# A four-layer GNN stack on one core: when the first layer's norms come, batch norm's coefficients in pieces, and another instruction order

## The chip, the cores and the metric

The kernel runs on one core of one Trainium2 chip. The metric is the device time of one execution in microseconds (us). Engines are named as in the profile: PE is the matrix engine (TensorE) and PEld its weight loads, DVE is VectorE, ACT is ScalarE, POOL is GpSimd, and SP (SyncE) issues most of the DMA transfers.

## The reference

The input x has 128 graphs of 64 nodes with 256 features, in float32; all graphs share one adjacency matrix. Four layers follow one another, each with a residual and a layer norm around it:

```python
def reference(x, adj, ...):
    # layer 0: aggregation, 256 -> 512, batch norm, ReLU, 512 -> 256, batch norm
    x = _layernorm(x + _L0_gnn_ref(x, adj, W1, b1, g1, be1, W2, b2, g2, be2))
    # layer 1: Chebyshev convolution, attention with 4 heads, feed-forward (exact GELU)
    x = _layernorm(x + _L1_gnn_ref(x, adj, adj, ...))
    # layer 2: two graph convolutions, then LSTMs over windows of 1, 2, 3 and 4 nodes
    x = _layernorm(x + _L2_gnn_ref(x, adj, ...))
    # layer 3: graph attention
    return _layernorm(x + _L3_gnn_ref(x, adj, W, a))

def _L0_gnn_ref(features, A, W1, b1, g1, be1, W2, b2, g2, be2):
    ...
    agg = jnp.einsum('nm,bmd->bnd', A_hat, features)
    x = agg.reshape(-1, d)
    h = jax.nn.relu(_batchnorm(x @ W1.T + b1, g1, be1))     # mean and variance over all 8192 rows
    out = h @ W2.T + b2
    return _batchnorm(out, g2, be2).reshape(b, n, -1)
```

Batch norm needs the mean and variance of a feature over all 128 x 64 rows. So layer 0 has two points at which every block must be done before any can go on: bn1 (512 features) and bn2 (256 features).

## The kernel before

**Blocks and tiles.** The 128 graphs are cut into 16 blocks of 8 graphs, 512 rows each. A block's activations are one SBUF tile of 128 partitions by 1024 elements (x, `Xs[i]`; a second one is `Hs[i]`). All matrix products write to four PSUM tiles of 128x1024 (`PS`); eight temporary SBUF tiles of the same size (`mem`, in the profile t) are handed out and returned.

**Layer 0.** `first_block(i)` aggregates block i (L346), multiplies by W1 in two halves of 256 features (L370; a half is 8 records on PE), evicts each to SBUF with the bias on ACT (L589, L591) and takes batch statistics on DVE (L593). The 512 features are four chunks of 128; half 0 is chunks 0 and 1, half 1 chunks 2 and 3. `bn_coeffs` makes scale and shift of bn1 for all four chunks at once: an aggregate for each chunk (L548), an addition (L549), a power on POOL (L551) and three small DVE operations (L553 to L555). `second_block(i)` applies scale, shift and ReLU on ACT (`relu`, L601) and multiplies by W2. Block 0 does that plainly, feature chunk by feature chunk (L611). Blocks 1 to 15 use a scheme with seven half-size products in place of eight (L645), with differences and sums on DVE and POOL and copies out of PSUM on ACT (L657) between them (DVE L664, L668, L669). Then come the statistics for bn2 (L684), and bn2's coefficients.

**Join to layer 1.** `end_block(i)` applies bn2 on ACT (L746, four of 512 elements for two blocks), transposes the block back on PE (L364), adds x (DVE L754) and applies the layer norm: statistics on DVE (L290 to L292), a power on POOL (L313), a small DVE operation (`ln_nm`, L316) and four ACT operations (L319). `block(i)` is layer 1: aggregation (PE L346), a copy (ACT L768), the product by Wc (PE L382), an addition (DVE L777), a layer norm, three elementwise operations (DVE L781 to L783), transposes (PE L358), a copy (ACT L791), the products for Q, K and V (PE L370, L815), attention, and a feed-forward part. ACT switches function tables between exp (L861) and gelu (L935). `at_end` says how many end blocks stand ahead of each block; their order is `ends = (0, 1, 12, 13, 14, 15, 2, 3, ...)`.

**Layers 2 and 3.** `gcn_block(i)` does the two graph convolutions and the first LSTM. `unit` does an LSTM over windows of p = 2, 3 and 4 nodes. Products that depend only on the input are at L1081; the recurrent steps use the same scheme of seven products (L1153), in four stages for each gate, with ACT and DVE work between them (L1221). The last units use plain products (L1289, L1291). `last_block(i)` is graph attention and the output.

**What sets the order.** The order of instructions on PE, DVE, ACT and POOL is fixed when the kernel is built. Each part of the work is a Python generator that yields a step (engine, planned us, PSUM tiles and temporaries to take, and from when), and `flow` runs a planned clock over all the generators: it always emits the step whose planned start is the earliest. A step's margin is multiplied by a pseudo-random number that depends on the stretch of 50 us in which it falls, with one seed for each stretch in `DRAWS`:

```python
soon = max(t if r[6].urgent else t + margin.get(e, 0.0) * drawn(r[0][1], t), free[e])
...
end, now = when + us, when
```

So a planned cost or a draw that changes can change the order of everything after it. The emitted order is what the engines execute, each in its own queue; real waits come from the data.

## Time and profile before

| | |
|---|---|
| time, median of 3 runs (lowest to highest) | 2354.76 us (2354.64 to 2355.97) |
| the profiled execution: time, span | 2355.12 us, 2353.0 us |
| mean granted PE clock | 0.987 |
| PE, DVE, ACT, POOL busy | 2266.4, 1365.9, 1167.2, 435.4 us |
| instructions | 40443 |
| DMA | 57.88 MB, mean 25 GB/s |
| first half of layer 0, bn1, second half | to 149.1, 149.1 to 155.9, to 263.6 us |
| first L364 of layer 1's inputs, first L382 | 268.2, 280.4 us |
| last LSTM product | ends at 2294.85 us |

A line of the timeline gives start, duration, engine, line, operation, output from input, and how many records it joins; in brackets stands the idle time of the engine before it, and what released it. Most float32 products of this kernel leave two records. A stage's row (a window) gives its length, each engine's busy time in it, the mean granted clock of PE, the share of time in which the DMA engines were busy, and their GB/s. In the page's first line the percentages are shares of the span. The chain is the work that ended last, followed back through what released it.

### The profile page before, as it was taken

The page shows a single profiled execution, that of the slowest core. Times are in us where ns is not written, and L with a number is a line of the kernel's source. Part 1 is how long each engine was busy: PE and PEld are TensorE (multiplying, and loading weights), DVE is VectorE, ACT ScalarE, POOL GpSimd, SP SyncE. Part 2 cuts the span into 40 slices and gives each one's busy share as a digit, 9 for nine tenths or more (in the row PEclk, how much of TensorE's full clock was granted, in tenths as well). Part 3 has the DMA queues.
Part 4 walks back from the last instruction along what each step waited for, and adds up shares of the span by engine and source line. Part 5 has one row for each costly group of instructions (what it writes and reads, how often), then busy time and mean ns, then how long its engine had stood idle before and what let it go on. Part 6 is the DMA issues. An engine that isn't in the chain of part 4 may idle for free.

```text
span 2353.0 us, 40443 instructions
## 1 busy us (share of the span) xinstructions
PE 2266.4 (96%) x16916; PEld 1753.1 (75%) x16916; DVE 1365.9 (58%) x2865; ACT 1167.2 (50%) x2257; POOL 435.4 (19%) x322
## 2 busy tenths in 40 slices
PE   8989789999999999999999999999999999999996
PEld 4548666676666676667667888999988888978884
DVE  5557589666766556567544444454454655563567
ACT  2357465644454544445444444444444544653676
POOL 0011124221314224215120100011100111110112
PEclk9999899999999999999999999999999999999998
DMA  6100310000000000101000000000001001000111
GB/s 170 46 1 1 99 60 30 27 10 11 10 10 10 10 11 3 44 2 46 19 19 10 18 1 1 19 1 1 1 1 36 1 10 37 28 10 27 54 37 55
DMA packets 42632, 57.88 MB, mean 25 GB/s; under 512 B 6225, under 2 KB 35537, under 8 KB 42449
## 3 DMA queue, kind: packets, MB, share of 16 engines
q1 hardware_dynamic: 41344, 54.22, 7.2%
q8 instruction: 132, 2.16, 0.4%
q10 hardware_dynamic: 1104, 1.08, 0.1%
q14 instruction: 52, 0.42, 0.1%
HBM read 38.52 MB, written 16.78 MB: 23 GB/s over the span
## 4 chain that ended last, share of the span: by engine, by line
PE 80%; issue 8%; DVE 7%; ACT 4%; POOL 0%; DMA 0%; ACTq 0%; POOLq 0%; DVEq 0%
PE ps L1153 27%; PE ps L1081 14%; PE ps L370 11%; PE ps L382 6%; PE ps L945 4%; PE ps L645 3%; PE ps L346 2%; PE ps L815 2%; PE ps L1532 2%; PE ps L1289 2%; PE ps L1291 2%; PE ps L358 2%; DVE ln_st L290 1%; PE ps L364 1%; DVE ln_mv L291 1%
## 5 line engine op out<-in xcount | busy, mean ns | idle before, releaser
L1153 PE MATMUL ps<-t,x 128*128 128x256 f32 x928 | 226.8, 380 | 0.3 <-DVE x L1221 0.3
L313 POOL TENSOR_TENSOR ln_rs<-ln_rs,neghalf 128x4 f32<-128x4 f32 (+1 forms) x104 | 108.5, 1043 | 610.6 <-DVE ln_rs L292 535.6
L1153 PEld LDWEIGHTS ps<-t,x 128*128 128x128 f32 x928 | 173.0, 190 | 22.8 <-issue 1.6
L1049 ACT ACTIVATE t<-ps,bih 128x512 f32<-128x512 f32 (+5 forms) x185 | 98.2, 568 | 159.7 <-PE ps L1081 103.7
L319 ACT ACTIVATE x<-x,ln_nm,ln_rs 128x256 f32<-128x256 f32 x228 | 118.1, 591 | 66.9 <-DVE ln_nm L316 66.9
L1153 PE MATMUL ps<-x,x 128*128 128x256 f32 x608 | 147.5, 380 | 1.5 <-DVE t L1221 1.1
L1049 ACT ACTIVATE x<-ps,bih 128x512 f32<-128x512 f32 (+5 forms) x159 | 82.2, 548 | 106.3 <-PE ps L1081 67.9
L1153 PEld LDWEIGHTS ps<-x,x 128*128 128x128 f32 x608 | 114.4, 190 | 17.2 <-DVE t L1221 1.8
L370 PE MATMUL ps<-t,W1T 128*128 128x512 f32 x256 | 114.7, 595 | 0.0
L290 DVE BATCH_NORM_STATS2 ln_st<-x 128x6 f32<-128x256 f32 x244 | 97.6, 400 | 0.7
L1049 ACT ACTIVATE x<-x,bih 128x512 f32<-128x512 f32 (+5 forms) x134 | 69.3, 564 | 51.8 <-DVE x L1219 49.7
L1081 PE MATMUL ps<-t,wL 128*128 128x512 f32 x216 | 94.6, 594 | 0.2 <-ACT t L1378 0.2
L291 DVE BATCH_NORM_AGGREGATE ln_mv<-ln_st 128x2 f32<-128x6 f32 x448 | 81.4, 182 | 15.3
L1081 PE MATMUL ps<-h,wL 128*128 128x192 f32 (+2 forms) x456 | 89.6, 352 | 0.6 <-DVE x L1599 0.6
L1081 PE MATMUL ps<-h,x 128*128 128x256 f32 x384 | 86.1, 379 | 0.0
L370 PEld LDWEIGHTS ps<-t,W1T 128*128 128x128 f32 x256 | 46.7, 190 | 48.9 <-issue 48.5
L1081 PEld LDWEIGHTS ps<-h,wL 128*128 128x128 f32 x456 | 69.6, 190 | 17.8 <-issue 16.0
L1212 DVE COPY x<-ps 128x256 f32<-128x256 f32 (+2 forms) x67 | 25.5, 381 | 98.4 <-PE ps L1153 98.4
L1219 DVE TENSOR_TENSOR x<-ps,x 128x512 f32<-128x512 f32 (+2 forms) x67 | 40.8, 609 | 69.3 <-PE ps L1153 64.3
L316 DVE SCALAR_TENSOR_TENSOR ln_nm<-ln_mv,ln_rs 128x4 f32<-128x4 f32 (+1 forms) x104 | 61.4, 593 | 33.2 <-POOL ln_rs L313 33.1
L1081 PEld LDWEIGHTS ps<-h,x 128*128 128x128 f32 x384 | 72.8, 190 | 9.8
L319 ACT ACTIVATE t<-t,ln_nm,ln_rs 128x256 f32<-128x256 f32 x112 | 58.5, 591 | 41.0 <-DVE ln_nm L316 40.9
(692 smaller groups left out, 5374.3 us busy)
## 6 DMA issues: line engine op xcount, KB each, us to landing
t<-in_x_dram SPq DMA_DIRECT2D x28, 512.0 KB, 4.4
xd<-x SPq DMA_DIRECT2D x16, 512.0 KB, 2.6
x<-xd SPq DMA_DIRECT2D x8, 512.0 KB, 3.3
out_dram<-x SPq DMA_DIRECT2D x8, 512.0 KB, 2.9
wL<-in_L_gnn_Wih_dram SPq DMA_DIRECT2D x2, 1024.0 KB, 4.9
x<-in_L_gnn_Whh_dram SPq DMA_DIRECT2D x2, 1024.0 KB, 5.0
wB<-in_L_gnn_W_dram SPq DMA_DIRECT2D x2, 512.0 KB, 4.3
h<-in_x_dram SPq DMA_DIRECT2D x2, 512.0 KB, 4.0
```

The costliest lines, as they stand in the source:

```text
L290: V.bn_stats(st[:, t, :], y[:, t, :])
L291: V.bn_aggr(mv[:, t, :], st[:, t, :])
L313: G.tensor_tensor(rs, rs, neghalf[:, :n], ALU.pow)
L316: V.scalar_tensor_tensor(nm, mv[:, :, 0], -1.0, rs, ALU.mult, ALU.mult)
L319: S.activation(y[:, t, :], y[:, t, :], AF.Identity, scale=rs[:, t : t + 1], bias=nm[:, t : t + 1])
L370: T.matmul(ps[:, c, :], w[:, k, (off + c) * P : (off + c + 1) * P], yT[:, k, :], start=(k == 0), stop=(k == nk - 1),)
L382: T.matmul(ps[:, t, :], yT[:, k, t * P : (t + 1) * P], w[:, k, :], start=(k == 0), stop=(k == nk - 1),)
L645: T.matmul(dst, w[:, k, :], y[:, k, :], start=first and k == 0, stop=k == 1, skip_group_check=not first)
L945: T.matmul(tm(PS[ps])[:, t, :], fm(mem[gs[k // 2]])[:, k % 2, t * P : (t + 1) * P], W2[:, k, :], start=(k == 0), stop=(k == 3),)
L1049: S.activation(dst, z, AF.Tanh, bias=bl[:, p - 1, 2 * g + c : 2 * g + c + 1], scale=(1.0 if g == 2 else 0.5) * (1.0 if p == 1 else 0.5),)
L1081: T.matmul(spread(fm(PS[ps])[:, j, :n], q), WL[p][0][:, k, m], x_of(0, q)[:, k], start=(k == 0), stop=(k == 1),)
L1153: T.matmul(dst, WS[p][name](k, g), y[:, k], start=first and k == 0, stop=k == 1, skip_group_check=not first)
```

## The change

It touches the order in five ways, and the arithmetic of no result. bn1's coefficients are made in two pieces, each as soon as the statistics of its two chunks are there; block 0's ReLUs are planned in pairs, and the other blocks' ReLUs, differences and evictions in smaller steps. (bn2 uses the same function with one piece, and the last block's statistics for it are single steps.) Fifteen of the sixteen blocks leave `end_block` without their layer norm, which is the first thing that `block(i)` then does; block 0 keeps it in `end_block` (`NORMED = range(1)`). Four end blocks in place of two stand ahead of block 0. Planned costs are changed in many steps, and steps that read PSUM are planned from the end of the product, or of the copy, that they wait for. `DRAWS` has 50 other values.

In the kernel before, one function makes all coefficients; after, this one is called for `(0, 2)` and `(2, 4)` of bn1 and `(0, 2)` of bn2:

```diff
+        def bn_coeffs(name, c0, c1, st, g, be, at):
+            sc, sh, mv = (t[:, c0:c1] for t in bn[name])
+            for c in range(c1 - c0):
+                yield step("V", 0.5, at=lambda: at(c0 + c))
+                V.bn_aggr(mv[:, c, :], st[:, c0 + c, :, :].rearrange("p i s -> p (i s)"))
+            yield step("V", 0.2)
             V.tensor_scalar(sc, mv[:, :, 1], EPS, None, ALU.add)
             yield step("G", 1.0)
-            G.tensor_tensor(sc, sc, neghalf[:, :nch], ALU.pow)
+            G.tensor_tensor(sc, sc, neghalf[:, : c1 - c0], ALU.pow)
             yield step("V", 0.6)
...
+        stats_at = lambda c: ready(*[("l0a", c // 2, i) for i in blocks])
+        for c in (0, 2):
+            tasks.append(
+                (
+                    lambda c=c: stats_at(c),
+                    lambda c=c: bn_coeffs("bn1", c, c + 2, st1, cols["g1"], cols["be1"], stats_at),
...
+        tasks += [(lambda i=i: ready(("bn1", 0), *[("bn1", 2)] * (i > 0)), lambda i=i: second_block(i), 2) for i in blocks]
```

In `second_block`:

```diff
             if i == 0:
                 for f in range(4):
-                    yield step("S", 0.7)
-                    relu(f)
-                    yield step("T", 1.75, ps=int(f == 0), waits=f == 3)
+                    if f % 2 == 0:
+                        for j in (f, f + 1):
+                            t_j = yield step("S", 0.65, at=lambda: done.get(("bn1", f)))
+                            relu(j)
+                    yield step("T", 1.75, ps=int(f == 0), at=t_j - 0.65 * (1 - f % 2))
...
-            yield step("S", 2.92)
-            for f in range(4):
-                relu(f)
+            t_x = yield step("S", 1.46)
+            relu(0)
+            relu(1)
...
-            yield step("S", 0.75, waits=False)
+            t = yield step("S", 0.75, at=max(t, t_2))
             S.copy(y[:, 0, :], p[:, 0, :])
             S.copy(y[:, 3, :], p[:, 3, :])
-            t = yield step("T", 1.75)
+            yield step("T", 1.75, at=max(t, t_h))
             product(A12, h[:, :, u], p[:, 2, :])
```

At the join to layer 1:

```diff
     def end_block(i):
...
-        yield step("S", 1.5)
         for c in range(2):
+            yield step("S", 0.7)
...
-        yield from ln_steps_act(x)
+        if i in NORMED:
+            yield from ln_steps_act(x)
         mark("end", i)
 
     def block(i):
         x = X[i]
         mark("begun", i)
+        if i not in NORMED:
+            yield from ln_steps_act(x)
...
-    at_end = {0: 2, 1: 4, 2: 8, 3: 10, 4: 14, 5: 16}
+    at_end = {0: 4, 1: 4, 2: 8, 3: 10, 4: 14, 5: 16}
```

Planned costs and waits, of which these are the LSTM's main ones:

```diff
-        us = n * 1.68e-3
-        v_us, g_us, s_us = (0.08 + n * r for r in (1.15e-3, 2.4e-3, 1.05e-3))
+        us = 0.012 + n * 1.665e-3
+        v_us, g_us, s_us = (0.08 + n * r for r in (1.15e-3, 2.35e-3, 1.0e-3))
+        v2_us, s2_us = 0.07 + n * 2.25e-3, 0.2 + n * 1.68e-3
...
-                at[g, "a"] = yield step("S", copy_us, at=t - us, waits=False)
+                at[g, "a"] = yield step("S", copy_us, at=t, waits=False)
                 S.copy(y[:, 0, :], v[:, 0, :])
...
-                yield step("T", us, at=h_at, waits=False)
+                yield step("T", us, at=max(h_at, at[g, "a"], at[g, "e"]), waits=False)
                 product(g, "A12", h_u, v[:, 2, :])
...
-                at[g, "0"] = yield step("V", two_us, at=at[g], waits=False)
+                at[g, "0"] = yield step("V", two_us, at=t, waits=False)
                 V.tensor_tensor(y[:, 0:2, :], v[:, 2:4, :], y[:, 0:2, :], ALU.add)
```

The rest changes a planned number alone (0.95 to 0.98 for the aggregations, and the gates', for example), or the ordering key `tbl`.

More of the change, by code (lines that the diff above doesn't have):

```diff
@@ L31 @@
 STRETCH = 50.0
-DRAWS = [511, 307, 323, 0, 388, 0, 0, 35, 178, 58, 461, 150, 363, 205, 36, 263, 190, 963, 453, 309, 108, 239, 50, 391, 578, 171, 630, 639, 804, 485, 290, 771, 646, 0, 976, 942, 0, 370, 0, 0, 618, 674, 887, 378, 432, 790, 44, 487, 800, 1]
+DRAWS = [119, 456, 684, 0, 152, 590, 97, 0, 0, 316, 775, 750, 291, 668, 396, 690, 972, 316, 700, 299, 810, 345, 289, 861, 902, 463, 567, 883, 455, 277, 848, 910, 108, 288, 531, 607, 103, 756, 415, 205, 829, 978, 419, 437, 870, 596, 976, 248, 270, 919]
 @with_exitstack
@@ L313, in ln_steps_act @@
         G.tensor_tensor(rs, rs, neghalf[:, :n], ALU.pow)
-        yield step("V", 0.2)
+        yield step("V", 0.2, tbl="m")
         nm = sm.tile([P, n], F32, tag="ln_nm", name="ln_nm")
@@ L539, in eig, with bn_tiles @@
             PS.give(0)
-        def bn_coeffs(name, nch, st, g, be):
-            mv = ctile([P, nch, 2], f"{name}mv")
-            sc = ctile([P, nch], f"{name}sc")
-            sh = ctile([P, nch], f"{name}sh")
-            yield step("V", 0.15 + 0.5 * nch)
-            for c in range(nch):
-                V.bn_aggr(mv[:, c, :], st[:, c, :, :].rearrange("p i s -> p (i s)"))
+        def bn_tiles(name, nch):
+            bn[name] = ctile([P, nch], f"{name}sc"), ctile([P, nch], f"{name}sh"), ctile([P, nch, 2], f"{name}mv")
+        def bn_coeffs(name, c0, c1, st, g, be, at):
[4 more added lines that the diff above has]
+            yield step("V", 0.2)
             V.tensor_scalar(sc, mv[:, :, 1], EPS, None, ALU.add)
             yield step("G", 1.0)
-            G.tensor_tensor(sc, sc, neghalf[:, :nch], ALU.pow)
+            G.tensor_tensor(sc, sc, neghalf[:, : c1 - c0], ALU.pow)
             yield step("V", 0.6)
-            V.tensor_tensor(sc, sc, g, ALU.mult)
+            V.tensor_tensor(sc, sc, g[:, c0:c1], ALU.mult)
             V.tensor_tensor(sh, mv[:, :, 0], sc, ALU.mult)
-            V.tensor_tensor(sh, be, sh, ALU.subtract)
-            bn[name] = sc, sh
-            mark(name)
+            V.tensor_tensor(sh, be[:, c0:c1], sh, ALU.subtract)
+            mark(name, c0)
         st1 = ctile([P, 4, NBLK, 6], "st1", wp)
@@ L569, in first_block @@
                 xs = early[i]
-            yield step("T", 0.95, ps=1, sl=1, tbl="quarter")
+            yield step("T", 0.98, ps=1, sl=1, tbl="quarter")
             ps = PS.take()
@@ L593, in first_block @@
                     V.bn_stats(st1[:, 2 * hf + c, i, :], dst[:, c, :])
-            mark("l0a", i)
+                mark("l0a", hf, i)
         def second_block(i):
-            sc1, sh1 = bn["bn1"]
+            sc1, sh1, _ = bn["bn1"]
             src = [(fm(Xs[i]) if f < 2 else H[i])[:, f % 2, :] for f in range(4)]
@@ L623, in second_block @@
                 return
-            yield step("S", 2.92)
-            for f in range(4):
-                relu(f)
+            t_x = yield step("S", 1.46)
+            relu(0)
+            relu(1)
             x, h = fm(Xs[i]), H[i]
             u, v = slice(0, TB // 2), slice(TB // 2, TB)
-            yield step("V", 1.4, sl=2, tbl="m")
+            t_1 = yield step("V", 0.7, sl=2, at=t_x, tbl="m")
             slots = [mem.take() for _ in range(2)]
@@ L636, in second_block @@
             V.tensor_tensor(T1, x[:, :, v], x[:, :, u], ALU.subtract)
-            V.tensor_tensor(T2, h[:, :, v], T1, ALU.subtract)
-            yield step("G", 1.3, waits=False, tbl="m")
-            G.tensor_tensor(T4, h[:, :, u], T2, ALU.subtract)
-            yield step("V", 0.7, tbl="m")
-            V.tensor_tensor(T3, h[:, :, v], x[:, :, v], ALU.subtract)
+            t_h = yield step("S", 1.46, at=t_x)
+            relu(2)
+            relu(3)
             def product(w, y, dst, first=False):
@@ L649, in second_block @@
             A11, A12, A22 = (W2T[:, k : k + 2, c * P : (c + 1) * P] for k, c in ((0, 0), (2, 0), (2, 1)))
-            yield step("T", 1.75, ps=1)
+            t = yield step("T", 1.75, ps=1, at=t_1)
             ps = PS.take()
@@ L654, in second_block @@
             product(W2S[0], T1, p[:, 3, :], first=True)
-            yield step("S", 0.75, waits=False)
+            t_2 = yield step("V", 0.7, at=t_h, tbl="m")
+            V.tensor_tensor(T2, h[:, :, v], T1, ALU.subtract)
+            yield step("G", 1.3, waits=False, tbl="m")
+            G.tensor_tensor(T4, h[:, :, u], T2, ALU.subtract)
+            yield step("V", 0.7, tbl="m")
+            V.tensor_tensor(T3, h[:, :, v], x[:, :, v], ALU.subtract)
+            t = yield step("S", 0.75, at=max(t, t_2))
             S.copy(y[:, 0, :], p[:, 0, :])
             S.copy(y[:, 3, :], p[:, 3, :])
-            t = yield step("T", 1.75)
+            yield step("T", 1.75, at=max(t, t_h))
             product(A12, h[:, :, u], p[:, 2, :])
@@ L669, in second_block @@
             V.tensor_tensor(y[:, 0:2, :], p[:, 2:4, :], y[:, 0:2, :], ALU.add)
-            yield step("T", 0.88)
+            t_y = Clock.end + LAG
+            t = yield step("T", 0.88)
             product(A22, T4, p[:, 0, :])
@@ L673, in second_block @@
                 mem.give(sl)
-            yield step("S", 1.5, ps=-1)
+            t_h = yield step("S", 0.6, at=t_y)
             S.activation(h[:, 0, :], fm(Xs[i])[:, 0, :], AF.Identity, bias=cols["b2"][:, 0:1])
+            if i == NBLK - 1:
+                yield step("V", 0.65, waits=False)
+                V.bn_stats(st2[:, 0, i, :], h[:, 0, :])
+                mark("l0b", 0, i)
+            yield step("S", 0.4, at=t_y)
             S.activation(h[:, 1, v], y[:, 3, :], AF.Identity, bias=cols["b2"][:, 1:2])
+            yield step("S", 0.4, ps=-1, at=t)
             S.activation(h[:, 1, u], p[:, 0, :], AF.Identity, bias=cols["b2"][:, 1:2])
@@ L681, in second_stats @@
         def second_stats(i):
-            yield step("V", 1.25)
-            for c in range(2):
+            for c in range(i == NBLK - 1, 2):
+                yield step("V", 0.65)
                 V.bn_stats(st2[:, c, i, :], H[i][:, c, :])
-            mark("l0b", i)
+                mark("l0b", c, i)
         blocks = range(NBLK)
@@ L689 @@
         tasks[3:3] = [(None, later_loads, 0)]
-        tasks.append(
-            (
-                lambda: ready(*[("l0a", i) for i in blocks]),
-                lambda: bn_coeffs("bn1", 4, st1, cols["g1"], cols["be1"]),
-                0,
-            )
-        )
-        tasks += [(lambda: ready(("bn1",)), lambda i=i: second_block(i), 2) for i in blocks]
-        tasks.append(
-            (
-                lambda: ready(*[("l0b", i) for i in blocks]),
-                lambda: bn_coeffs("bn2", 2, st2, cols["g2"], cols["be2"]),
-                0,
-            )
-        )
+        bn_tiles("bn1", 4)
+        bn_tiles("bn2", 2)
+        stats_at = lambda c: ready(*[("l0a", c // 2, i) for i in blocks])
[4 more added lines that the diff above has]
+                    lambda c=c: bn_coeffs("bn1", c, c + 2, st1, cols["g1"], cols["be1"], stats_at),
+                    0,
+                )
+            )
+        tasks += [(lambda i=i: ready(("bn1", 0), *[("bn1", 2)] * (i > 0)), lambda i=i: second_block(i), 2) for i in blocks]
+        ends_at = lambda c: ready(*[("l0b", c, i) for i in blocks])
+        tasks.append((lambda: ends_at(0), lambda: bn_coeffs("bn2", 0, 2, st2, cols["g2"], cols["be2"], ends_at), 0))
         flow([Stream(1, 0, [(None, eig, 0)], urgent=True), Stream(6, 1, tasks)], {"T": 2.0})
@@ L731 @@
         V.tensor_tensor(rb2, rb2, be2, ALU.add)
-    sc2, sh2 = bn["bn2"]
+    sc2, sh2, _ = bn["bn2"]
     Wv_par = Wv.rearrange("p k (u r e) -> p k r u e", u=2, r=2)
+    NORMED = range(1)
     def end_block(i):
@@ L762, in block @@
         mark("begun", i)
-        yield step("T", 0.95, ps=1, sl=1, tbl="quarter")
+        if i not in NORMED:
+            yield from ln_steps_act(x)
+        yield step("T", 0.98, ps=1, sl=1, tbl="quarter")
         ps = PS.take()
@@ L829, in block @@
         G.tensor_tensor(y, y, row["bo"], ALU.add)
-        yield step("T", 0.95, ps=1, sl=1, tbl="quarter")
+        yield step("T", 0.98, ps=1, sl=1, tbl="quarter")
         ps = PS.take()
@@ L879, in block @@
         PS.give(ps)
-        yield step("T", 0.95, ps=1, sl=1, tbl="quarter")
+        yield step("T", 0.98, ps=1, sl=1, tbl="quarter")
         ps = PS.take()
@@ L1090, in gates @@
         def gates(pair, t, ps, sl):
-            t = yield step("S", 0.1 + n * 2.5e-3, ps=-1, at=t, waits=False)
+            t = yield step("S", 0.42 + n * 1.64e-3, ps=-1, at=t, waits=False)
             for j, (g, c) in enumerate(pair):
@@ L1147, in lstm @@
         hn = n // 2
-        half_us, two_us = (0.15 + j * hn * 1.05e-3 for j in (1, 2))
+        half_us, two_us = (0.07 + j * hn * 1.08e-3 for j in (1, 2))
         copy_us = 0.15 + hn * 1.0e-3
@@ L1226, in stage4 @@
                 product(g, "A22", T4, v[:, 0, :])
-                yield step("S", 0.1 + n * 1.15e-3, at=at[g, "0"], waits=False)
+                yield step("S", 0.1 + n * 1.03e-3, at=at[g, "0"], waits=False)
                 gate(of(act[g])[:, 0], of(act[g])[:, 0], g, 0)
@@ L1243, in lstm @@
             yield from stage4(2)
-            t_g = yield step("V", 2 * v_us, at=at[2], waits=False, tbl="m")
+            t_g = yield step("V", v2_us, at=at[2], waits=False, tbl="m")
             times(of(act[2]), of(act[0]), of(act[2]))
@@ L1251, in lstm @@
             yield from stage4(1)
-            yield step("V", 2 * v_us, at=at[1], waits=False, tbl="m")
+            yield step("V", v2_us, at=at[1], waits=False, tbl="m")
             times(cell, of(act[1]), cell)
             mem.give(act[1])
-            t = yield step("V", 2 * v_us, at=t_g, waits=False, tbl="m")
+            t = yield step("V", v2_us, at=t_g, waits=False, tbl="m")
             V.scalar_tensor_tensor(cell, cell, 0.5, of(act[2]), ALU.mult, ALU.add)
@@ L1259, in lstm @@
                 mem.give(j)
-            t = yield step("S", 2 * s_us, at=t, waits=False)
+            t = yield step("S", s2_us, at=t, waits=False)
             S.activation(of(act[2]), cell, AF.Tanh, scale=0.5)
-            t = yield step("V", 2 * v_us, at=max(t, at[3]), sl=0 if last else 1, waits=False, tbl="m")
+            t = yield step("V", v2_us, at=max(t, at[3]), sl=0 if last else 1, waits=False, tbl="m")
             if last:
@@ L1291, in products @@
                         T.matmul(dst, WL[p][1][:, k, m], of(s_h)[:, k], start=False, stop=(k == 1))
-                t = yield step("S", 0.3 + n * 2.1e-3, ps=-1, at=t, waits=False)
+                t = yield step("S", 0.42 + n * 1.64e-3, ps=-1, at=t, waits=False)
                 for j, (g, c) in enumerate(pair):
@@ L1331, in gcn_block @@
     def gcn_block(i):
-        yield step("T", 0.95, ps=1, sl=1, tbl="quarter")
+        yield step("T", 0.98, ps=1, sl=1, tbl="quarter")
         ps = PS.take()
@@ L1353, in gcn_block @@
         S.activation(mem[s_h1], mem[s_h1], AF.Relu)
-        yield step("T", 0.95, ps=1, sl=1, tbl="quarter")
+        yield step("T", 0.98, ps=1, sl=1, tbl="quarter")
         ps = PS.take()
@@ L1713 @@
         MARGIN,
-        start=done["bn2",],
+        start=done["bn2", 0],
     )
```

## The prediction

> **What bounds the kernel now.** I read the page first, then PE's waits, then a table of stages, then the timeline at the two joins of layer 0.

> ```profile
> PE 2266.4 (96%) x16916; PEld 1753.1 (75%) x16916; DVE 1365.9 (58%) x2865; ACT 1167.2 (50%) x2257; POOL 435.4 (19%) x322
> ...
> PE 80%; issue 8%; DVE 7%; ACT 4%; POOL 0%; DMA 0%; ACTq 0%; POOLq 0%; DVEq 0%
> ```

> TensorE (PE) is the bound: 96% busy, and 80% of the chain that ends last. No other engine passes 58% of the span. The change keeps every matmul, so it can only move the 86.6 us of PE idle time and the few us lost at half clock. The stage table says where the idle time lies (span minus PE busy in each stretch).

> ```profile
> core 0: us, PE busy (x) PEld busy (x) DVE busy (x) ACT busy (x) POOL busy (x), PEclk, DMA share, GB/s
> 149.10:168.00 18.90, 10.30 (x26) 5.28 (x26) 10.04 (x19) 14.27 (x22) 5.66 (x4) 0.82 0.01 1
> 258.70:323.10 64.40, 44.09 (x395) 32.14 (x393) 46.11 (x118) 35.94 (x59) 12.46 (x14) 0.76 0.26 84
> 1240.00:1750.00 510.00, 507.53 (x2825) 457.59 (x2824) 236.44 (x441) 218.19 (x499) 49.11 (x39) 1.00 0.02 6
> 1750.00:2294.90 544.90, 526.15 (x3078) 463.11 (x3076) 296.45 (x748) 293.63 (x720) 68.12 (x67) 1.00 0.08 26
> 2294.90:2353.00 58.10, 38.83 (x309) 28.36 (x308) 43.63 (x163) 37.58 (x111) 13.04 (x19) 0.84 0.17 55
> ```

> The two joins of the change, bn1 (149–168) and layer 0 to layer 1 (259–323), idle 8.6 and 20.3 us, with a reduced clock besides. The second LSTM stretch idles 18.8, the tail 19.3, the head 7.3, all else 12.3. PE's timeline at the joins (start, duration, then in brackets the idle time before and its releaser):

> ```profile
> 155.86 5.77 PE L611 MATMUL ps<-x,W2T 128*128 128x512 f32 x8 [6.72 <-ACT x L601]
> ...
> 261.92 1.64 PE L645 MATMUL ps<-t,W2T 128*128 128x256 f32 x4 [1.21 <-DVE x L669]
> 268.20 0.47 PE L364 MATMUL ps<-ident,h 128*128 128x128 f32 x1 [4.64 <-ACT h L746]
> ...
> 276.44 2.82 PE L346 MATMUL ps<-LnT,x 64*64 64x64 f32 x64 [4.07 <-ACT x L319]
> 280.39 6.59 PE L382 MATMUL ps<-wA,t 128*128 128x256 f32 x16 [1.13 <-ACT t L768]
> ...
> 289.81 3.62 PE L382 MATMUL ps<-wA,t 128*128 128x256 f32 x16
> ...
> 301.50 1.94 PE L358 MATMUL ps<-ident,t 128*128 128x128 f32 x8 [6.33 <-DVE ln_nm L316]
> ```

> The first L382 takes 6.59 us, the second, of equal work, 3.62: the clock was at half in 280.4–286.2 (granted 0.50).

> **bn1 in two pieces.** The 6.72 us before L611 are one chain: last eviction L589, two statistics, then

> ```profile
> 151.10 1.91 DVE L548 BATCH_NORM_AGGREGATE bn1mv<-st 128x2 f32<-128x96 f32 x4
> ...
> 155.00 2.22 ACT L601 ACTIVATE x<-x,bn1sh,bn1sc 128x512 f32<-128x512 f32 x3 [4.55 <-DVE bn1sh L555]
> ```

> with POOL's power (1.01) and three small DVE operations between. Call P the end of the last L370 product, 149.14. In the new order both blocks 14 and 15 do their first half before their second, so chunks 0 and 1 have their statistics two products of 3.44 us earlier (eight records of 0.43 each; L611's records run at that cadence at full clock). Their coefficients come at about P−2, before the last eviction ends (P+1.3). ReLU and handover (0.86 us from L601's start to L611) start PE at P+2.2: idle 2.2 in place of 6.72. Features 0 and 1 keep PE until P+5.6. The second piece has two aggregates fewer ahead of it (0.96 us), so its first ReLU starts at P+4.9 and PE goes on at P+5.8: idle 0.2. Features 2 and 3 (3.44) and the first two products of blocks 1 and 2 (3.44) follow, to P+12.6. Then ACT is late: from P+4.9 its new queue holds ten ReLUs (0.71 each), two evictions of block 0 (1.3 together) and two copies (0.6 together), so the next product starts at P+14.1, after 1.5 more of idle. By then 10.3 us of work are done and 3.8 lost. Before, 6.9 were done at P+17.8 (166.96, where PE resumes after a wait of 1.89 for ACT) and 10.9 lost: 8.6 idle, 2.3 at half clock (granted 0.51 in 156–160). The gain is 7.1 if nothing else is late. I take off 1.1 for the clock, which costs 2.0 if it halves after the shorter holes too (four us at 0.51, as before): **−6**, bounds −8 and −3 (ACT late once more: it was busy in 14.27 of these 18.9 us). The price is four more DVE operations (0.17 and 3×0.16) and one POOL power (1.01), under PE's last products.

> **Second half of layer 0, bn2.** Products that depend on each other through one PSUM tile stand further apart in the new order (21 gaps under two products' time, 1.72 us, before; 11 after). This stretch idles 1.9 in all: **−0.5**, bounds −1.5 and +0.5. bn2's pieces bring nothing: in the order both aggregates still stand behind both last statistics of block 15. The last products now come back to back behind DVE's additions (L668, L669: 0.42 and 0.68), which I count at 6.65 idle where 0.52, 1.21 and 4.64 stood: **+0.3**, bounds −1 and +2.

> **Join to layer 1.** Four end blocks (0, 1, 12, 13) stand before block 0, not two, and only block 0 has its norm there. On DVE the additions of blocks 1, 12 and 13 (1.22 each) are now queued around block 0's statistics: one before them, two between them and ln_nm, which else waits 1.2 for POOL. Block 0's norm is late by 1.2 plus about 1.3, and transposes that run longer add some tenths: L346 starts near 279.6, not 276.44, a loss of 3.2. The idle time before it does not grow as much, since PE has 16 more transposes then. L382 of block 0 follows at 283.5 and ends at 290.1 at half clock, as before. Then the other end pays. The 6.33 us before L358 contain the statistics of blocks 12 and 13 (DVE 292.96–297.6), and ACT's norm of block 12 (2.08) stood before block 0's copy L791. Both are gone from there: after L382 I count on DVE L777, the statistics, L754 of blocks 14 and 15, block 1's L777 (which needs its own L382, done at 296.7), then L781–783 (3×1.22), and L358 at 301.9. PE has by then also transposed blocks 2 and 3 (2.0 us, at 314.3 and 321.0 before): idle 3.2, not 6.33. If the clock stays up, the Q and K products end at 311.1; before, with those transposes, 316.3: −5.2. If it falls as before (granted 0.50 in 302–310, 3.4 us lost), −1.8. **−3.5**, bounds −9 (the early phase too at full clock) and +3 (DVE's queue worse than counted).

> On the clock: it halved at about 262.3, after holes of only 0.52 and 1.21 us among short work, so a hole of 3.2 is no safe one. [...]

> The 12 other norms moved to the start of their blocks put some 4.5 us (271.95 to 276.44: statistics, POOL, ln_nm, L319) ahead of each block's L346. Cover is the other blocks in flight, six at a time. In layer 1 after 323 PE idles 4.7 and 1.9 us with just such chains inside each block, so **0**; uncovered, each would cost 4.5. SP issues eight loads of x in a row instead of six; the join's transfers of weights come behind them, with DMA at 0.78 in 268–272, and no row of PE waits for them: 0.

> **ACT's tables.** The new order switches between exp and gelu in smaller groups: 27 table loads, not 19.

> ```profile
> L935 ACT ACT_TABLE_LOAD x9 | 11.5, 1283 | 8.0 <-PE ps L370 7.8
> ```

> Eight more are 10.3 us of ACT, in a layer where ACT is half idle and the work behind these loads waited for them 1.3 us in all: **+0.5**, bounds 0 and +10.3. [...]

> **Head, LSTM, tail.** L346 of block 0 now stands before L489, which waited 1.3 for DVE: **−1**, bounds −1.5 and 0. In the LSTM the planner's prices are the same work in another order. I laid each dependent chain's durations (from these rows) against the PE work queued between its ends: the shortfall from 330 on is 9.1 us before, 9.9 after, with more at 1700–2180 (6.0, not 3.5), and the table hides what queues do. **+1.7**, bounds −8 and +10, which span about a third of the 27.9 idle us there. In the tail, PE work behind the last plain LSTM product falls from 33.2 to 28.1 us, so that product ends 5.1 later against an end set by DVE (43.6 of 58.1 busy). DVE has 43.2 us queued behind its last LSTM step, not 45.8, and ACT 35.4, not 38.9: **+1**, bounds −1 and +4.

> **Sum:** −1−6−0.5+0.3−3.5+0.5+1.7+1 = −7.5. The profiled execution took 2355.12 (span 2353.0, 2.1 around it), 0.36 above the median; it goes to 2347.6, the median to 2347.3.

> **Rivals.** *Slower: the redrawn order loosens the LSTM.* Two neighbouring LSTM stretches idle 2.5 of 510 and 18.8 of 544.9 us (0.5% and 3.5%), with the same products; only order differs. If the first got the second's share, it would idle 17.6: +15.1 for my +1.7, the sum +5.9, time 2360.7. It decides from 12.2 us above my terms on. For it: the rise I count at 1700–2180. Against: equal spacing of the L1153 products overall (104 gaps under 1.72 us before, 103 after).
> *No change.* The clock falls at both joins (bn1 −3, join 0), ACT's tables cost 2 and the tail +3: −1+−3−0.5+0.3+0+2+1.7+3 = 2.5, about 2357; with one of these as I have it, 2352 to 2354.
> *Larger gain: the LSTM tightens.* If the second stretch reaches the first's 0.5% (2.7 idle), −16.1 for +1.7: 2329.5; half of that gives some 2338.

> **Chances.** Forecast (2340 to 2352) 0.62; slower rival 0.10; no change 0.18; larger gain 0.10. About 0.2%, 4.7 us, is what a measurement here can tell. The forecast's part below 2350.0, 0.58, and the larger gain make 0.68 faster; 0.22 same; 0.10 slower. The range takes in the upper half of the larger gain and all of no change but its end: 2336 to 2356.

> **What would show it.** Right: PE's wait at the first W2 product near 2 us, not 6.7; L346 of block 0 some 3 us later than before, counted from the end of layer 0; the wait before L358 near 3; stretches after 323 within 10 us of 27.9 idle. Wrong: granted clock at half through the Q and K products, waits at exp or gelu with L945 or L898 behind them, or new waits of over 10 us among the L1153 products.

## The result

The changed kernel takes 2321.52 us (median of four runs, 2320.32 to 2324.77), the kernel before 2355.11 beside it: a ratio of 0.9859, 95% interval 0.9843 to 0.9874. That is 33.6 us faster, where 7.5 were forecast, and below the range of 2336 to 2356. The profiled execution took 2324.77 us and was the slowest of the four; its span is 30.2 shorter than before, so the traces show 30.2 of the 33.6. The page's lines that answer to those of before:

```profile
span 2322.8 us, 40477 instructions
...
PE 2256.3 (97%) x16916; PEld 1753.1 (75%) x16916; DVE 1333.9 (57%) x2869; ACT 1176.4 (51%) x2265; POOL 436.8 (19%) x323
```

PE is still the bound; its idle time fell from 86.6 to 66.5 us, and it is busy 10.1 us less on as many records, in part since less of the work ran at half clock (mean granted clock 0.990, before 0.987). PE's timeline at the two joins:

```profile
150.44 5.40 PE L615 MATMUL ps<-x,W2T 128*128 128x512 f32 x8 [2.05 <-ACT x L603]
155.67 3.60 PE L615 MATMUL ps<-h,W2T 128*128 128x512 f32 x8
...
162.61 1.13 PE L647 MATMUL ps<-h,W2T 128*128 128x256 f32 x4
...
248.93 2.12 PE L647 MATMUL ps<-t,W2T 128*128 128x256 f32 x8 [0.19 <-DVE x L677]
256.04 0.47 PE L364 MATMUL ps<-ident,h 128*128 128x128 f32 x1 [4.99 <-ACT h L762]
257.45 5.02 PE L364 MATMUL ps<-ident,h 128*128 128x128 f32 x31 [0.94 <-ACT h L762]
267.35 2.82 PE L346 MATMUL ps<-LnT,x 64*64 64x64 f32 x64 [4.87 <-ACT x L319]
271.30 6.75 PE L382 MATMUL ps<-wA,t 128*128 128x256 f32 x16 [1.13 <-ACT t L787]
...
289.56 1.06 PE L358 MATMUL ps<-ident,t 128*128 128x128 f32 x8 [3.31 <-DVE t L802]
291.72 10.21 PE L370 MATMUL ps<-t,wA 128*128 128x512 f32 x16 [1.10 <-ACT t L810]
```

Read the brackets: 2.05 in place of 6.72 at bn1, and then no wait for ACT (1.89 before); 4.87 and 3.31 in place of 4.07 and 6.33 at the join. The last line is a product at half clock (granted 0.51 in 291 to 298): 10.21 us for 6.9 us of work.

To set the two orders against each other I cut both traces where PE has done the same work (each record counted at the distance between equal records at full clock, 0.43 us for 512 columns, 0.22 for 256). The rows of this stage table are such stretches of the changed kernel, roughly; 148.4 to 160.6, bn1, has about the work that 149.1 to 168.0 had, 248.2 to 308.1 that of 258.7 to 323.1, and so on. The second row ends about 1.1 us too late for equal work, so the table of terms below, which goes by the exact cuts, has 1.3 us more gain there than its length shows, and less on either side.

```profile
148.40:160.60 12.20, 10.16 (x23) 5.07 (x24) 5.47 (x12) 9.66 (x15) 1.67 (x2) 0.86 0.01 1
248.20:308.10 59.90, 43.37 (x379) 32.08 (x381) 41.70 (x94) 31.95 (x49) 10.72 (x12) 0.80 0.35 107
1731.00:2210.20 479.20, 471.76 (x2729) 419.91 (x2728) 258.77 (x614) 252.86 (x617) 58.08 (x54) 1.00 0.07 23
2210.20:2322.80 112.60, 91.95 (x652) 72.08 (x650) 79.72 (x291) 76.58 (x213) 23.15 (x32) 0.91 0.18 57
```

The same work as in the third, the late part of the LSTM, took 495.0 us before (1750 to 2245). The last row of each table is the tail:

```profile
1750.00:2245.00 495.00, 476.25 (x2757) 421.77 (x2756) 263.36 (x632) 258.16 (x629) 59.77 (x56) 1.00 0.07 24
2245.00:2353.00 108.00, 88.73 (x630) 69.70 (x628) 76.72 (x280) 73.05 (x204) 21.39 (x30) 0.91 0.15 50
```

So the late LSTM stretch is 15.8 us shorter and idles 7.4, not 18.8. The forecast's terms beside what the cut traces give:

| stretch of equal PE work (before) | forecast | measured |
|---|---|---|
| to the end of layer 0's first half (149.1) | −1 | −1.1 |
| bn1 (149.1 to 168) | −6 | −6.8 |
| second half of layer 0 (to 258.7) | −0.5 | −2.4 |
| bn2 and join (to 323.1) | −3.2 | −5.8 |
| layer 1 (to 1240), tables with it | +0.5 | −3.0 |
| LSTM (to 2245) | +1.7 | −15.6 |
| tail | +1 | +4.4 |
| sum | −7.5 | −30.3 |

Up to the join the hand count was 5.4 short; behind it, it missed 17.4 and the sign.

### The profile page after: what moved, and what is told of

Its sections match the earlier page's. It is cut to its first block, busy times and chain, and to the rows that moved or that the text cites. A ratio compares the mean times of both kernels' runs of the same rounds, so it can differ in the third digit from the quotient of the medians.

```text
span 2322.8 us, 40477 instructions
## 1 busy us (share of the span) xinstructions
PE 2256.3 (97%) x16916; PEld 1753.1 (75%) x16916; DVE 1333.9 (57%) x2869; ACT 1176.4 (51%) x2265; POOL 436.8 (19%) x323
## 5 line engine op out<-in xcount | busy, mean ns | idle before, releaser
L1173 PE MATMUL ps<-x,x 128*128 128x256 f32 x832 | 204.5, 379 | 0.0
L1173 PE MATMUL ps<-t,x 128*128 128x256 f32 x736 | 179.0, 380 | 0.8 <-DVE t L1232 0.8
L1069 ACT ACTIVATE x<-ps,bih 128x512 f32<-128x512 f32 (+5 forms) x185 | 95.6, 553 | 151.3 <-PE ps L1101 98.5
L1173 PEld LDWEIGHTS ps<-x,x 128*128 128x128 f32 x832 | 156.0, 190 | 18.7
L1173 PEld LDWEIGHTS ps<-t,x 128*128 128x128 f32 x736 | 138.2, 190 | 20.3 <-DVE t L1232 1.2
L1069 ACT ACTIVATE t<-ps,bih 128x512 f32<-128x512 f32 (+5 forms) x151 | 79.5, 563 | 127.2 <-PE ps L1101 85.0
L319 ACT ACTIVATE x<-x,ln_nm,ln_rs 128x256 f32<-128x256 f32 x212 | 110.2, 593 | 45.1 <-DVE ln_nm L316 44.6
L370 PE MATMUL ps<-t,W1T 128*128 128x512 f32 x256 | 115.3, 595 | 0.0
L291 DVE BATCH_NORM_AGGREGATE ln_mv<-ln_st 128x2 f32<-128x6 f32 x448 | 81.6, 182 | 15.3
L290 DVE BATCH_NORM_STATS2 ln_st<-x 128x6 f32<-128x256 f32 x224 | 89.7, 401 | 0.3
L1101 PE MATMUL ps<-t,wL 128*128 128x512 f32 x192 | 83.9, 593 | 1.2 <-ACT t L897 1.2
L1101 PEld LDWEIGHTS ps<-h,wL 128*128 128x128 f32 x456 | 70.0, 190 | 17.4 <-issue 16.7
L370 PEld LDWEIGHTS ps<-t,W1T 128*128 128x128 f32 x256 | 46.4, 190 | 47.5 <-issue 47.3
L1101 PEld LDWEIGHTS ps<-h,x 128*128 128x128 f32 x384 | 72.8, 190 | 10.4 <-issue 0.5
L1239 DVE TENSOR_TENSOR x<-ps,x 128x512 f32<-128x512 f32 (+2 forms) x71 | 42.4, 598 | 51.5 <-PE ps L1173 41.4
L319 ACT ACTIVATE t<-t,ln_nm,ln_rs 128x256 f32<-128x256 f32 x104 | 54.2, 593 | 32.5 <-DVE ln_nm L316 32.5
L1101 PEld LDWEIGHTS ps<-t,wL 128*128 128x128 f32 x192 | 36.3, 190 | 44.7 <-issue 42.6
```

The lines of the kernel that those rows point to most:

```text
L290: V.bn_stats(st[:, t, :], y[:, t, :])
L291: V.bn_aggr(mv[:, t, :], st[:, t, :])
L319: S.activation(y[:, t, :], y[:, t, :], AF.Identity, scale=rs[:, t : t + 1], bias=nm[:, t : t + 1])
L370: T.matmul(ps[:, c, :], w[:, k, (off + c) * P : (off + c + 1) * P], yT[:, k, :], start=(k == 0), stop=(k == nk - 1),)
L1069: S.activation(dst, z, AF.Tanh, bias=bl[:, p - 1, 2 * g + c : 2 * g + c + 1], scale=(1.0 if g == 2 else 0.5) * (1.0 if p == 1 else 0.5),)
L1101: T.matmul(spread(fm(PS[ps])[:, j, :n], q), WL[p][0][:, k, m], x_of(0, q)[:, k], start=(k == 0), stop=(k == 1),)
```

## The experiments

Two theories stood at first. A: truer planned costs and waits make a better order. B: the fifty draws were fitted to just these costs, and any edit spoils the fit. For each run I give the time, its ratio to the kernel before run beside it, and the time lost (elapsed less PE work) up to PE work 265, which is just behind the join, and from there to PE's last record. These are 69.5 and 149.9 us for the kernel before, 52.0 and 135.5 for the changed one. They hold more than idle time (half clock too, and what short products take beyond the distance they are counted at) and leave out the output behind PE's last record, some 8 to 13 us, so only their differences are read, and two of them can differ by less or more than the times do.

**The LSTM's edits and the draws, one at a time.** `e1` is the changed kernel with all edits between L1061 and L1312 undone, and one aggregation's planned cost in `gcn_block` with them; `e2` is the kernel before with these alone; `e3` and `e4` exchange the draws:

```diff
-DRAWS = [119, 456, 684, 0, 152, ...]    # e3: the changed kernel; e4: the other way round
+DRAWS = [511, 307, 323, 0, 388, ...]
```

> The changed kernel with the old planned costs and waits in the LSTM (all edits from L1061 to L1312 undone); its draws, its layer 0 and its join stay. The order is the changed kernel's up to the first LSTM gates. Theory A (truer costs and waits make a better order): the late LSTM stretch idles some 19 us again instead of 8, time 2331 to 2338, and everything before 1200 us stays. Theory B (the fifty draws were fitted to these very costs, any edit spoils the fit): both LSTM stretches and layer 1 get worse, 2335 to 2350. If the planner's costs do not matter at all: 2319 to 2326.

> The kernel before with the change's LSTM edits alone (planned costs, and waits on PSUM), its own draws. Theory A: the late LSTM stretch falls from 18.8 us of idle to about 8, time 2340 to 2346. Theory B: the draws no longer fit, no gain or a loss, 2353 to 2370.

> The changed kernel with the fifty draws of before, costs and waits as changed. Theory A: the gain of the joins and of the LSTM stays, 2320 to 2330. Theory B: joins keep their 10 to 12 us, the LSTM and layer 1 give back their 18: 2335 to 2350.

> The kernel before with the fifty new draws and nothing else. Theory A: no gain, within 6 of before, 2349 to 2362. Theory B, fit to these costs: worse, 2355 to 2375. If the new draws are simply better ones whatever the costs: 2338 to 2346.

| run | time | ratio (95%) | lost to 265 | behind |
|---|---|---|---|---|
| e1 | 2391.93 | 1.0152 (1.0135 to 1.0169) | 51.5 | 201.6 |
| e2 | 2367.08 | 1.0045 (1.0030 to 1.0060) | 69.0 | 157.2 |
| e3 | 2354.39 | 0.9994 (0.9985 to 1.0004) | 51.3 | 163.2 |
| e4 | 2389.87 | 1.0142 (1.0127 to 1.0157) | 67.2 | 183.9 |

B's signs came in all four, in e1, e3 and e4 beyond its sizes. Neither half of the change gains behind the join without the other: in whole times, the LSTM's costs alone cost 12 us, the draws alone 35, the draws without those costs 70 over the changed kernel, and e3, with every edit and the old draws, loses 163.2 us there where the kernel before loses 149.9. Up to the join it is otherwise: with either set of draws the changed planner loses 51 to 52 us, the old one 67 to 70. That part belongs to the edits.

**No draws, and random ones.** How the two sets of draws were found is not on record; that each is good with its own planner alone says that they were fitted to it. If both sets are fits, the planners must be compared without them: `DRAWS = []`, and twice fifty random numbers.

> The changed kernel with an empty list of draws: every margin at its full value, no fit at all. To be read against the kernel before treated alike (the next run). Theory C (the edits fix the joins for about 15 us, and what lies behind the join is the fit): 13 to 18 us faster than that one, all of it before PE work 265, the later stages alike within 10. Theory D (truer costs and waits also order the LSTM better without a fit): 25 us faster or more, with the later stages at least 10 better.

> The kernel before with an empty list of draws. By both theories slower than before, since its own draws were fitted too: 2365 to 2395; the joins as before (bn1 idle 6.7, the wait before L358 some 6).

> The changed kernel with fifty random draws, fitted to nothing. Theory E (so far: the edits make a planner whose unfitted orders are about 15 us better behind the join, and both fits take some 26 off that): time lost behind PE work 265 about 160 us (as with no draws, 160.2), some 15 below the kernel before with the same draws (next run); 2350 to 2362. Theory C (behind the join all is luck and fit): that difference lies anywhere within 12 either way of zero.

> The kernel before with the same random draws. Theory E: 2370 to 2390, with some 175 us lost behind PE work 265. Theory C: 2365 to 2385, about 160 to 165 lost there.

> The changed kernel with a second set of fifty random draws. Theory E (unfitted orders of the changed planner are better behind the join; so far by 10 and by 41 us): 155 to 180 us lost behind PE work 265, and 10 to 40 below the kernel before with the same draws (next run); 2350 to 2380. If the two pairs were luck: the two kernels within 10 there, apart by the 10 to 17 us of the joins alone.

> The kernel before with that second set. Theory E: 175 to 215 us lost behind PE work 265, 2380 to 2430. If luck: 155 to 180 lost, 2365 to 2390.

| draws | changed: time, lost to 265, behind | before: time, lost to 265, behind |
|---|---|---|
| none (e5, e6) | 2357.43, 57.2, 160.2 | 2375.16, 67.3, 170.1 |
| random 1 (e9, e10) | 2370.21, 61.5, 171.0 | 2430.53, 81.6, 212.1 |
| random 2 (e17, e18) | 2364.55, 63.8, 168.4 | 2405.60, 74.8, 191.3 |

The changed planner wins each pair, by 18, 60 and 41 us: 10 to 20 up to the join, 10, 41 and 23 from there to PE's last record. The first pair alone lies between C and D (a time difference of 17.7, as C had it, but half of it behind the join). C's bound of 12 either way is passed in the two random pairs, so C falls; three pairs of one sign are not many, though, and E missed both times of the first random pair (2350 to 2362 and 2370 to 2390 were expected) and hit those of the second. The fit is worth about as much to either: the three unfitted orders average 2364.1 and 2403.8 us, the fitted ones 2321.5 and 2355.1, so 43 and 49 us.

**Which edits behind the join.** The LSTM's edits taken out of the changed kernel and put alone into the one before, with no draws (`e11`, `e12`) and with the first random set (`e14`, `e13`):

> The changed kernel without its LSTM edits, no draws: to be read against the changed kernel without draws (160.2 us lost behind PE work 265, 2357.4). If the LSTM's costs and waits are what makes unfitted orders better: about 10 worse, 2364 to 2372. If the rest of the change does it (costs of the aggregations, the join, the norms): 2353 to 2361.

> The kernel before with the LSTM edits alone, no draws: to be read against the kernel before without draws (170.1 us lost behind PE work 265, 2375.2). If the LSTM edits make better orders: about 10 faster, 2360 to 2369. If not: 2371 to 2380.

> The kernel before with the LSTM edits alone and the same random draws as in the pair of runs with random draws (before: 212.1 us lost behind PE work 265; changed: 171.0). Theory F (the LSTM's new planned costs and waits are what makes the unfitted orders better): 160 to 190 lost there, 2375 to 2405. If the pair's difference came from the rest of the change: 200 to 220 lost, 2415 to 2440.

> The changed kernel without its LSTM edits, the same random draws. Theory F: 190 to 220 us lost behind PE work 265, 2385 to 2420. If the rest of the change carries it: 160 to 180, 2360 to 2380.

| lost behind 265 | before | before + LSTM edits | changed − LSTM edits | changed |
|---|---|---|---|---|
| no draws | 170.1 (2375.16) | 158.8 (2364.74) | 194.5 (2391.73) | 160.2 (2357.43) |
| random 1 | 212.1 (2430.53) | 188.6 (2401.20) | 181.2 (2375.13) | 171.0 (2370.21) |

The LSTM edits gain in all four comparisons: 11, 34, 24 and 10 us. The rest of the change is +24 and −31 without them, +1 and −18 with them: no sign to be read. e12 and e13 came as expected if the LSTM edits carry the gain; e11 lost three times what was expected, and e14 is a miss for theory F: its time lies in the rival's range.

**Waits or durations.** `e15` takes the three planned waits on PSUM back and keeps the durations, `e16` the reverse, both from the changed kernel without draws:

```diff
-                at[g, "a"] = yield step("S", copy_us, at=t, waits=False)
+                at[g, "a"] = yield step("S", copy_us, at=t - us, waits=False)
...
-                yield step("T", us, at=max(h_at, at[g, "a"], at[g, "e"]), waits=False)
+                yield step("T", us, at=h_at, waits=False)
...
-                at[g, "0"] = yield step("V", two_us, at=t, waits=False)
+                at[g, "0"] = yield step("V", two_us, at=at[g], waits=False)
```

> The changed kernel with the three planned waits on PSUM of the LSTM's stages taken back (first copy from the end of its product's pair, A12 behind both copies, the two-quarter addition behind S3), its planned durations kept, no draws. With both kinds of edit 160.2 us are lost behind PE work 265, with neither 194.5. If the waits carry it: 180 to 200 lost, 2378 to 2398. If the durations do: 155 to 170, 2352 to 2368.

> The changed kernel with the LSTM's planned durations of before, its three planned waits on PSUM kept, no draws. If the durations carry it: 180 to 200 us lost behind PE work 265, 2378 to 2398. If the waits do: 155 to 170, 2352 to 2368.

e15 took 2371.05 us, e16 2371.33, with 173.2 and 172.5 lost: each edit alone brings most of the way from 194.5, and neither expectation came clean. They work in different stretches. In the LSTM (same work as 1240 to 2245 before) the changed kernel without draws takes 1004.2 us, without the new waits 1015.9, without the new durations 1000.6, without both 1021.6; the kernel before without draws 1013.5, with the LSTM edits 1003.4. So without draws every order with the waits lies at 1000 to 1004 and every one without at 1013 to 1022. With the first random set that does not repeat: 999.0 and 1023.8 with them, 1005.7 and 1017.7 without. There the LSTM edits made the LSTM of the kernel before 18.1 us longer (1023.8 for 1005.7), and their gain of 24 came in layer 1 and the tail. So what they improve is not the LSTM in every order; only the sign of the whole repeats.

In the changed kernel without draws the durations act in layer 1, and there by one collision. PE's waits in layer 1 of e16 and, with the same length, of e11:

```profile
PE ps L893 <- POOL t L886: 10.9, 1, 10.9
PE ps L893 <- POOL h L886: 2.9, 1, 2.9
```

These 13.8 us are nearly all of the 15 by which those two exceed e15 and e5 in layer 1 (936.2 and 935.9 us against 921.2 and 920.7). PE had come to the transposes of the last block's attention weights with nothing else queued, while subtraction, exp, sums and POOL's product for them were still to do. Not worse everywhere, then, but one chain uncovered: the kernel before without draws, which has the old durations, takes 920.8 there, and 920.7 with the LSTM edits.

**The joins, one part at a time.** `e7` makes bn1's coefficients in one piece, and sets the planned clock back behind layer 0, so that PE's order behind the join is the changed kernel's:

```diff
-        for c in (0, 2):
+        for c in (0,):
...
-                    lambda c=c: bn_coeffs("bn1", c, c + 2, st1, cols["g1"], cols["be1"], stats_at),
+                    lambda c=c: bn_coeffs("bn1", 0, 4, st1, cols["g1"], cols["be1"], stats_at),
...
+    shift = done["bn2", 0] - 256.61    # taken off done and off the times of free tiles
```

> The changed kernel with bn1's coefficients in one piece, called for all four chunks; the planned clock is set back afterwards so that the order behind the join stays. If the early piece is what closes the hole, PE's wait at the first W2 product goes from 2.05 to 5.4, and the time rises by 3.4, or by 5.1 if one more window runs at half clock: 2324.5 to 2327. If the gain at bn1 came from the other edits (ReLUs in pairs, first products of two blocks in a row), under 2 us: 2320 to 2323.5.

```profile
153.23 6.43 PE L615 MATMUL ps<-x,W2T 128*128 128x512 f32 x8 [5.83 <-ACT x L603]
```

2331.77 us, ratio 0.9898 (0.9883 to 0.9912), 10.3 over the changed kernel's median and above the expected range; the two profiled spans are 5.4 apart. The wait is back (5.83), bn1 takes 16.6 us, not 12.1, and the clock was at half for 6.83 us, not 3.41. Another 2.5 went in the second half of layer 0, where waits return (L647 for DVE's L677 1.9, for ACT's L665 1.1). The profiles show half of the 10.3: the changed kernel's profiled execution lies 3.3 above its median, that of e7 1.7 below. What makes one execution of a kernel slower than another stays open. Behind PE work 265 it loses 135.2 us, against 135.5: with PE's order kept, those 2000 us of kernel repeat to 0.3.

`e8` takes the join back, all norms in the end block and two end blocks first:

```diff
-    NORMED = range(1)
+    NORMED = range(NBLK)
...
-    at_end = {0: 4, 1: 4, 2: 8, 3: 10, 4: 14, 5: 16}
+    at_end = {0: 2, 1: 4, 2: 8, 3: 10, 4: 14, 5: 16}
```

> The changed kernel with the join as before: all sixteen blocks with their norm in the end block, two end blocks ahead of block 0, not four. Layer 0 stays. If the join's 4 to 6 us are these edits', the waits of before come back there (some 6 us at L358, L364 of blocks 2 and 3 behind it), 4 to 6 us lost at the join; if they came from elsewhere, the join stays within 2. The order behind it changes too, and with it the fit: Theory C has the whole at 2330 to 2360.

2382.86 us, ratio 1.0115 (1.0100 to 1.0130). It loses 9.2 more up to PE work 265, where 4 to 6 were expected, and 47.7 more behind it, where the fit is gone. PE's timeline at its join:

```profile
268.03 4.78 PE L346 MATMUL ps<-LnT,x 64*64 64x64 f32 x128 [6.68 <-ACT x L319]
...
290.32 1.94 PE L358 MATMUL ps<-ident,t 128*128 128x128 f32 x8 [6.36 <-DVE ln_nm L316]
```

Both holes of the old join are there, and the first is longer than it was. But the short wait at L358 is no property of the new join alone: with the old draws (e3), and with none (e5), the changed planner too makes PE wait there, 6.77 us for ln_nm. Over all orders run, the stretch of PE work 215 to 265 loses 29.4 to 37.1 us with the new join and 35.5 to 40.4 with the old.

## Why the prediction was wrong

**Right: bn1.** Idle 2.05 where 2.2 was counted, the second piece's first ReLU at P+4.6 where P+4.9 was (153.02, last L370 at 148.38), 6.8 gained for 6. The clock did halve after the shorter hole, for 3.4 us (granted 0.50 in 151.18 to 154.59), and hid ACT's lateness: PE was still at the first products when ACT was ready (162.61, no wait). That it halved does not follow from the hole's length, as the last section shows: in e3 the same hole left it up (granted 1.00 in 149.47 to 152.89), and the stretch took 10.4 us, not 12.1.

**Right: the mechanics of the join.** From the end of layer 0 to L346 of block 0: 16.3 us against 12.9, 3.4 later where 3.2 was counted; the wait before L358 3.31 where 3.2 was. The clock fell (granted 0.50 in 291.12 to 297.95), the branch priced at −1.8, and the end of Q and K gives −2.0 (50.7 us from layer 0's end in both, with two blocks' transposes more done). The rest of the stretch's 5.8 lies at bn2 (2.2, counted at +0.3; the hole of 1.21 is gone) and behind Q and K (1.6).

**Short: the second half of layer 0.** −0.5 stood for −2.4. Its idle time nearly vanished, and it did in most orders of the changed planner: PE work 142 to 215 loses 0.2 us without draws and with either fitted set, 2.8 and 6.3 with the random ones, against 1.3 to 5.5 with the old planner.

**Wrong: the term for the LSTM, and with it layer 1.** The step that failed is "the planner's prices are the same work in another order", +1.7 with bounds −8 and +10. Measured were −15.6 in the LSTM, −3.0 in layer 1, +4.4 in the tail. The count behind it set each dependent chain against the PE work queued between its ends. That finds no chain that waits in ACT's or DVE's queue behind another's work. Such waits made most of the late stretch's idle time: PE's waits over 0.2 us there sum to 18.5 us, and 14.8 of them were ended by an operation that followed another on its engine without a pause. After, it is 3.4 of 7.0. (In some of these the operation ahead can belong to the same chain; the count does not part them.) PE's longest waits there, before:

```profile
PE ps L1153 <- DVE t L1221: 2.9, 2, 1.8
PE ps L364 <- ACT h L1580: 1.5, 1, 1.5
PE ps L1153 <- ACT h L1544: 1.4, 1, 1.4
```

and after:

```profile
PE ps L1309 <- DVE x L1523: 0.8, 1, 0.8
```

The longest of before, 1.8 us, on DVE and PE:

```profile
1828.52 0.42 DVE L290 BATCH_NORM_STATS2 ln_st<-x 128x6 f32<-128x256 f32 x1
...
1830.76 0.17 DVE L292 TENSOR_SCALAR ln_rs<-ln_mv 128x4 f32<-128x4 f32 x1
1830.84 0.30 DVE L1221 TENSOR_TENSOR t<-ps,t 128x144 f32<-128x144 f32 x1
...
1831.29 0.73 PE L1153 MATMUL ps<-x,wA 128*128 128x144 f32 x4 [1.82 <-DVE t L1221]
```

PE's last product ended at 1829.47. The LSTM's addition (L1221), for which PE waited, came at 1830.84, behind the nine operations of a layer norm's statistics that filled DVE from 1828.52 on.

After, no single wait in this stretch is longer than 0.8. The count also had this stretch get worse (6.0 for 3.5 at 1700 to 2180). Of the 15.8 us, 11.3 are idle time, 1.7 a period of half clock that is gone (3.41 us from 1832.47 on, granted 0.50), and the rest, 2.8, lies in time that the profile counts as busy and stays unexplained. The rival "the LSTM tightens" named this place, this sign and nearly this size (−16.1), at a chance of 0.10; the range took in half of it. (The measured stretch stopped at 1.5% of idle time, not 0.5%.) It rested on what the trace did show, two neighbouring stretches of the same products at 0.5% and 3.5% idle: order alone is worth that much here.

What the runs put in the term's place: the new order is a pair, planner and draws. The LSTM edits gained 10 to 34 us behind the join wherever no fit was lost, and cost 7 where one was (e2); a fit is worth 43 to 49 us over the unfitted average. So neither explains the 14 us behind the join alone: with the old draws the changed planner has none of them (e3), with the new draws the old planner has none (e4). How they divide between better planning and a better fit stays open: both fits may not be equally good, and orders scatter by tens.

**Not tested alone: the tables.** 27 loads of 1283 ns are there, and layer 1 is 3.0 us shorter all the same, so nothing like the upper bound of 10.3 shows; what the eight loads cost cannot be told apart from the order. In 23 of the 27 the next operation on ACT started 11 or 12 ns behind the load, so there the trace shows nothing beyond the 1283 ns. ACT still stood idle for PE ahead of them, 13.4 us in all at L954:

```profile
L954 ACT ACT_TABLE_LOAD x13 | 16.7, 1283 | 13.6 <-PE ps L370 13.4
```

**Tail:** +4.4 for +1, and out of bounds by 0.4. A new wait of 3.9 us (PE L364 for ACT's L1512) goes with it; what brought it was not tested.

## What to carry to other kernels

Where a join is bound by one chain, a hand count along the queues came within a us: of what is ready, in which queue it stands, and what goes before it. Where a planner writes the order, price the edit and the order apart: compare the planners with the same unfitted draws, several of them, and give the order a range as wide as two like stretches of the trace differ. And keep the order fixed behind the edit when one part is tried, as e7 did; otherwise a lost fit of 40 us covers an effect of 5.

## What the hardware showed that I had not expected

What went with a fall was how much of one such stretch of 3.41 us PE was busy. The stretch that ends with the fall at the changed kernel's bn1, and the one that holds most of an equally long hole (2.05 us) in e3, where the clock stayed up:

```profile
147.77:151.18 3.41, 1.36 (x4) 0.49 (x3) 2.04 (x4) 2.66 (x4) 0.00 (x0) 1.00 0.00 0
149.47:152.89 3.42, 1.65 (x4) 0.87 (x5) 2.39 (x5) 3.42 (x6) 0.44 (x1) 1.00 0.00 0
```

PE was busy for 40% of the first and 48% of the second. So equally long holes went either way, and no row that the prediction had could tell it where the hole would lie against the steps. I laid such stretches over the traces of the kernel before and of the changed one, each from its fall at bn1, from 20 to 2300 us. At full clock the clock fell after 10 of 1311 stretches. In nine of them PE was busy for 0 to 40%, in the tenth for 49.5%: that is the fall at 262.34 in the kernel before, where holes of 0.52 and 1.21 us left PE busy for 1.69 us of 3.41. After the other 1301, with PE busy for 50.3% or more, it stayed up. The 48% of e3, without a fall, lie below the tenth, so near one half the share alone did not tell. Four of the ten stretches were idle; in the other six PE was busy for 26 to 49.5%.

The fall comes at such a stretch's end, 2.8 us (after) and 4.0 us (before) behind PE's last work at bn1. After, that was 0.7 us after PE had resumed, and at L370 it was 1.6 us after L358 had begun: a short hole was paid for when it was over.

At half clock, in the same two traces and bounds, the clock came back after all ten stretches in which PE was busy for 86% or more, and after none of the twelve with 83% or less: the periods of two or three stretches are those with pauses in them. In the kernel before, PE was busy for 2.82 us, then 2.44, then all of the three stretches from 276.0 on, and the clock came back at 286.24, 9.8 us after L346 of block 0 had started at 276.44.
